# A 2D Haar inverse, by rows: sixteen of 64 channels by TensorE products, forty-eight by VectorE butterflies

## The chip, the core and the metric

The kernel runs on one core of one Trainium2 chip. The metric is the device time of one execution in microseconds. Before the change the median of three runs is 2953.84 us (2952.67 to 2955.11).

## What is computed

The input is a batch of 4 images with 64 channels of 256 x 256 float32. Four layers follow one another: two long convolutions, a Haar layer, and a third long convolution. Cut to what matters:

```python
def conv(x, hx, hy, bias):            # layers 0, 1 and 3
    k = einsum('ijk,imk->ijmk', hx, hy)   # the 2D filter is a product of two 1D filters
    y = irfft2(rfft2(x, 512) * rfft2(k, 512) / 512)[..., :256, :256]
    return y + x * bias

def haar_layer(x, v, conv_w, tau):    # layer 2
    f1 = haar2d(x)                    # 1D Haar along rows, then along columns
    acc = 0
    for i in range(2):
        f4 = einsum('bchw,oc->bohw', f1 * v[i], conv_w[i])      # mixes the channels
        acc = acc + sign(f4) * relu(abs(f4) - tau[i])
    return haar2d(acc, inverse=True) + x
```

As each filter is a product of two 1D filters, the kernel computes a convolution as two products of an image with triangular Toeplitz matrices, one for each axis. hx and hy come from small sine networks.

## The kernel before, in words

**Stages.** A channel's image is a tile of 128 partitions x 512. For each batch the kernel does three things in turn.

1. Convolutions (function `convolutions`), one channel after another: load x and the Toeplitz tile `t` (L237), product `a0` (tile pa), ACT copy (L260), product `y0` (tile py), residual sum on DVE (L277), the same again for the second layer (`a1`, `y1`). Then `pairs` takes sums and differences of neighbouring columns (L322, L323), `store` keeps them in DRAM (`keep`), `levels` does the rest of the row transform, and `split`, `rest`, `down` and `away` do the column transform: an ACT copy rounds to float32r (L354), DVE subtracts for the remainder (L359), and TensorE multiplies both with a sign matrix (tile pz, L366). The result goes to DRAM (`coef`).
2. Mixing (function `mixing`), 64 groups g: load four coefficient rows of all channels, multiply with the channel matrix (tile px, L434), scale (L453 on DVE, L458 on ACT), absolute value (L462) and sign (L465) on ACT, threshold and product with the sign on DVE (L469, L473), and add (L479) into the large tile `z`. `z` is 128 partitions x (4 chunks of 16 channels) x 128 places x 16 channels; place_of gives the place of a row.
3. Inverse (function `inverse`): the column transform is done in place in `z` by butterflies on DVE. `halve` (L284, L285) subtracts and then forms 2 x even - odd; `level(n, chunk, ...)` does one level of one chunk of 16 channels, with n = 1, 2, 4, ..., 64; levels 32 and 64 are cut in parts of 16, so that a chunk has 7 wide pairs of 128x1024 (n = 16, two parts of 32, four of 64) and four narrow ones. Then for each channel c: `early` loads r from `keep` (L512) and the Toeplitz tile, `fetch` copies one channel out of `z` (tile zc, L519), `rows` multiplies and transposes (tile pw, L526, L527), `join` adds r and takes sums and differences (tiles t and u, L533, L536, L537), and the third convolution follows (`a3`, `y3` on tiles pa, py; output on ACT's DMA queue, L573). For batches 0 to 2, a third of the channels is put off: `aside` stores u in `late`, and `convolution` does them beside the mixing of batch 3.

**Order.** Nothing runs in loops over time. Each step of each unit is an event with a time in ticks (`at`), the tick of its unit plus an offset from the table `PLACE`; the events are sorted and issued in that order (L630). The tile framework then sets the final order on each engine by its own schedule, in which a later step can stand in a gap of its engine ahead of an earlier one, and it adds the waits. The convolutions of batch b+1 run beside the mixing of batch b; the inverse of batch b comes after its mixing, with the tail of the convolutions in it. In `inverse`, `along` is the first tick of the batch's mixing, `start` that of its inverse, and `turn` is 16 ticks ahead of the chunk's own first channel.

**Buffers.** PSUM: four banks of tag "mm" (pa, py, pz, pw) and two pairs for px. SBUF: five Toeplitz tiles, three of tag "f" (r, and the coefficient rows), two of tag "f4", two of tag "co" (y3 and the coefficients on their way out).

Of the kernel before, what the change touches and what calls it, by code (L numbers as in the profile page):

```python
# [9 lines left out]
F32 = mybir.dt.float32  # L10
F32R = mybir.dt.float32r
AF = mybir.ActivationFunctionType
ALU = mybir.AluOpType
# [3 lines left out]
B, C, S, EMB, ORD = 4, 64, 256, 33, 64  # L17
P = 128
# [7 lines left out]
PLACE = {  # L26
    "load": 0.714,
    "a0": 1.643,
    "a0 copy": 1.643,
    "y0": 2.571,  # L30
    "y0 sum": 2.571,
    "a1": 3.5,
    "a1 copy": 3.5,
    "y1": 4.429,
# [15 lines left out]
    "shrink": 1.777,  # L50
    "signed": 2.802,
    "add": 3.331,
    "early": -0.4,
    "fetch": 0.414,
    "rows": 1.071,
    "join": 1.433,
    "aside": 2.357,
    "a3": 2.47,
# [37 lines left out]
def conv_seq_kernel(ctx, tc, x, fz, fw, bias, decay, haar, haar_row, factors, vt, taut, wmix, out):  # L96
# [14 lines left out]
    nc = tc.nc  # L111

    const = ctx.enter_context(tc.tile_pool(name="const", bufs=1))
# [1 line left out]


    zpool = ctx.enter_context(tc.tile_pool(name="zpool", bufs=1))
    tp = ctx.enter_context(tc.tile_pool(name="toep", bufs=5))
    io = ctx.enter_context(tc.tile_pool(name="io", bufs=2))
    mx = ctx.enter_context(tc.tile_pool(name="mx", bufs=2))  # L120
    psm = ctx.enter_context(tc.tile_pool(name="psm", bufs=4, space=PSUM))
# [2 lines left out]

    hbt = const.tile([P, P], F32, name="hbt")
    hbr = const.tile([P, P], F32R, name="hbr")
    hrow = const.tile([P, 2, P], F32, name="hrow")
    hsinv, ident = hrow[:, 0, :], hrow[:, 1, :]
    wb = const.tile([P, 2, P], F32, name="wb")
# [3 lines left out]
    z = zpool.tile([P, 4, P, 4, 16], F32, name="z")  # L133
# [71 lines left out]
        return [load, *steps, end, warm]  # L205

    def constants():
        nc.sync.dma_start(hbt, haar)
        nc.sync.dma_start(hrow, haar_row)
        nc.vector.memset(wb, 0.0)  # L210
        for r in range(2):
            nc.sync.dma_start(wb[r * C : (r + 1) * C, r, :], wmix)
        nc.scalar.copy(hbr, hbt)
# [90 lines left out]
    def at(time, run, unit):  # L304
        events.append((time, len(events), run, unit))
# [104 lines left out]
    def mixing(b, start, n_act):  # L410

        st = {}

        def load(g):
            f = mx.tile([P, 2, S], F32, name=f"f_{b}_{g}", tag="f", bufs=3)
            nc.sync.dma_start(f, coef[b].rearrange("k c p w -> (k c) p w")[:, 2 * g : 2 * g + 2])
            st[g] = {"f": f}
            if g % GT == 0:
                t = mx.tile([P, 2, GT, 16], F32, name=f"vt_{b}_{g}", tag="vt")
                nc.sync.dma_start(t, scales[g // GT])  # L420
                st["vt", g // GT] = t

        def scale(g, i):
            return st["vt", g // GT][:, i, g % GT, :]

        def over(g, i, n):
            return scale(g, i)[:, :n].unsqueeze(2).to_broadcast([P, n, C])

        def mix(g):
            f = st[g]["f"]  # L430
            ps = psx.tile([P, 2, 2, S], F32, name=f"px_{b}_{g}", tag="mix")
            for q in range(2):
                for h in range(2):
                    nc.tensor.matmul(  # L434
                        ps[:, q, h, :],
                        f[:, q, h * P : (h + 1) * P],
                        wb.rearrange("p r n -> p (r n)"),
                        start=True,
                        stop=True,
                    )  # L440
            if g == 0:

                one, two = ps[:, 0, :, :P], ps[:, 0, :, P:]
                d = mx.tile([P, 2, P], F32, name=f"d_{b}", tag="mag")
                nc.vector.tensor_copy(d, two)
                nc.vector.tensor_sub(two, one, d)
                nc.vector.tensor_add(one, one, d)
            st[g]["f4"] = mx.tile([P, 16, C], F32, name=f"f4_{b}_{g}", tag="f4")
            st[g]["px"] = ps.rearrange("p q h (r i o) -> p (q h r i) o", r=2, i=2)

        def scaled(g):
            px, n = st[g]["px"], 16 - n_act
            nc.vector.tensor_tensor(st[g]["f4"][:, :n], px[:, :n], over(g, 0, n), ALU.mult)  # L453

        def scaled_too(g, half):
            px, f4 = st[g]["px"], st[g]["f4"]
            for j in range(16 - n_act + half * (n_act // 2), 16 - (1 - half) * (n_act - n_act // 2)):
                nc.scalar.mul(f4[:, j], px[:, j], scale(g, 0)[:, j : j + 1])  # L458

        def size(g):  # L460
            mag = st[g]["mag"] = mx.tile([P, 16, C], F32, name=f"mag_{b}_{g}", tag="mag")
            nc.scalar.activation(mag, st[g]["f4"], AF.Abs)  # L462

        def sign(g):
            nc.scalar.activation(st[g]["f4"], st[g]["f4"], AF.Sign)  # L465

        def shrink(g):
            mag = st[g]["mag"]
            nc.vector.tensor_sub(mag, mag, over(g, 1, 16))  # L469

        def signed(g):
            mag = st[g]["mag"]
            nc.vector.scalar_tensor_tensor(mag, mag, 0.0, st[g]["f4"], ALU.max, ALU.mult)  # L473

        def add(g):
            parts = st.pop(g)["mag"].rearrange("p (q x i) (n c) -> p q i x n c", q=2, i=2, n=4)
            for q in range(2):
                slot = place_of(2 * g + q)
                nc.vector.tensor_add(  # L479
                    z[:, :, slot].rearrange("p n x c -> p x n c"), parts[:, q, 0], parts[:, q, 1]  # L480
                )

        def place_of(i):

            n = 1 << i.bit_length() - 1 if i else P
            return (2 * (i - n) + 1) * (P // 2 // n) if i else 0

        for g in range(S // 4):
            for name, stage in zip(
                ("mix load", "mix", "scaled", "scaled too", "scaled rest", "size", "sign", "shrink", "signed", "add"),  # L490
                (
                    load,
                    mix,
                    scaled,
                    lambda g: scaled_too(g, 0),
                    lambda g: scaled_too(g, 1),
                    size,
                    sign,
                    shrink,
                    signed,  # L500
                    add,
                ),
            ):
                at(start + g + PLACE[name if b + 1 < B else "l " + name], stage, g)

    def inverse(b, start, put_off):

        st = {}

        def early(c):  # L510
            r = mx.tile([P, 2, 2, P], F32, name=f"r_{b}_{c}", tag="f", bufs=3)
            nc.sync.dma_start(r, keep[b][c])  # L512
            st[c] = {"r": r}
            if c not in put_off:
                st[c][2] = toeplitz(2, c, f"t2_{b}_{c}")

# [5 lines left out]
        def rows(c):  # L522
            a = st[c]["z"]
            ps = psm.tile([P, 2, 2, P], F32, name=f"pw_{b}_{c}", tag="mm")
            for m in range(2):
                nc.tensor.matmul(ps[:, 0, m, :], a[:, 0, m, :], hsinv, start=True, stop=True)  # L526
                nc.tensor.transpose(ps[:, 1, m, :], a[:, 1, m, :], ident)  # L527
            st[c]["pw"] = ps

        def join(c):  # L530
# [14 lines left out]
        def when(tick, n, chunk, *span):  # L545
            at(tick + PLACE["level"], lambda _: level(n, chunk, *span), 0)

        at(along + 11 + PLACE["level"], lambda _: butterfly(), 0)
        for chunk in range(4):
            beside = b + 1 < B or chunk == 0  # L550
            turn = start + 16 * (chunk - 1)
            for n in (1, 2, 4, 8):
                when(along + 12 + chunk if beside else turn, n, chunk)
            when(along + 22 + 2 * chunk if beside else turn + 1, 16, chunk)
            for i in range(2):
                when(along + 38 + 4 * chunk + 2 * i if beside else turn + 2 + 2 * i, 32, chunk, 16 * i, 16)
            for i in range(4):
                when(turn + 4 + 3 * i if chunk else along + 43 + 8 * i - (i == 3), 64, chunk, 16 * i, 16)

        for c in range(C):  # L560
            for name, stage in zip(("early", "fetch", "rows", "join"), (early, fetch, rows, join)):
                at(start + c + PLACE[name], stage, c)
            if c in put_off:
                at(start + c + PLACE["aside"], aside, c)
            else:
                for name, stage in zip(("a3", "a3 copy", "y3", "y3 sum", "out"), last(b, st)):
                    at(start + c + PLACE[name], stage, c)

    def last(b, st):
        return [  # L570
# [45 lines left out]
    start = ready + 3  # L616
# [12 lines left out]
        ahead = start - 3  # L629
    for _, _, stage, unit in sorted(events, key=lambda e: e[:2]):  # L630
        stage(unit)


def _haar_order():
# [101 lines left out]
```

## Time and profile before

| what | value |
|---|---|
| median of three runs | 2953.84 us |
| the profiled execution's own time | 2959.32 us |
| its span | 2957.5 us |
| PE busy | 2826.3 us (96%), 16438 matmuls |
| DVE busy | 2529.3 us (86%) |
| ACT busy | 2056.6 us (70%) |
| POOL busy | 361.2 us (12%) |
| DMA | 649.69 MB, mean 220 GB/s |
| mean granted clock of TensorE | 0.992 |
| mixing of batch 1 (first px to first zc) | 1096 to 1550 us |
| inverse of batch 1 (first zc to next px) | 1550 to 1767 us |

The span is the time from the first to the last instruction in the profile. Busy is the union of the instructions of an engine. A matmul's record lasts from its start to a modelled end and overlaps the next one, so busy PE is more than the work it does. A float32 product stands in the trace as two matmul records. A row of a group of instructions gives line, engine, operation, tiles, shapes, count, busy time, mean duration in ns, and the idle time of the engine ahead of it with what ended it. In a list of stretches the columns are from:to, length, then busy time and count of each engine, the granted clock, the share of the DMA engines and GB/s.

### The profile page before, as it was taken

How to read it: one execution, taken by the hardware profiler on the slowest of the kernel's cores; microseconds unless marked ns; L12 is line 12 of the kernel's file. 1: busy time of each engine (PE TensorE's matmuls, PEld its weight loads, DVE VectorE, ACT ScalarE, POOL GpSimd, SP SyncE). 2: the span in 40 equal slices, each digit the busy share in tenths (PEclk: the TensorE clock that was granted, in tenths of full speed). 3: DMA queues.
4: the chain of work that ended last, by engine and by line, in shares of the span. 5: the costliest groups of instructions: out<-in, count | busy, mean ns of one | idle time of the engine just before them, and what ended most of it. 6: DMA issues, size and time to landing. Idle time of an engine off the chain costs nothing. (4 is left out here: it accounts for less than half of the span.)

```text
span 2957.5 us, 52078 instructions
## 1 busy us (share of the span) xinstructions
PE 2826.3 (96%) x16438; PEld 2541.0 (86%) x16438; DVE 2529.3 (86%) x4287; ACT 2056.6 (70%) x4885; POOL 361.2 (12%) x644
## 2 busy tenths in 40 slices
PE   8999999999898899999998899999998899998999
PEld 6899998888787898898987798898987798877898
DVE  4655568999998679999998669999998679999986
ACT  2333338999894558999884558999884558887454
POOL 0111111311111001131211001131221000000000
PEclk9999999999999999999999999999999999999999
DMA  5877777666566786777676786777776797767777
GB/s 159 248 231 230 232 235 218 207 201 205 180 204 199 249 264 198 211 215 212 208 215 210 241 271 194 214 211 216 210 209 215 247 280 235 231 200 210 223 237 213
DMA packets 599222, 649.69 MB, mean 220 GB/s; under 512 B 48449, under 2 KB 516900, under 8 KB 598820
## 3 DMA queue, kind: packets, MB, share of 16 engines
q1 hardware_dynamic: 519716, 562.02, 65.0%
q10 hardware_dynamic: 79232, 84.34, 8.1%
q8 instruction: 133, 2.18, 0.3%
q14 instruction: 141, 1.16, 0.1%
HBM read 426.70 MB, written 219.48 MB: 218 GB/s over the span
## 5 line engine op out<-in xcount | busy, mean ns | idle before, releaser
L246 PE MATMUL py<-t,a 128*128 128x256 f32 x3072 | 927.7, 384 | 8.8 <-ACT a L260 8.3
L260 ACT COPY a<-pa 128x512 f32<-128x512 f32 x768 | 490.8, 639 | 482.4 <-PE pa L247 428.9
L458 ACT ACTIVATE f<-px,vt 128x64 f32<-128x64 f32 x2816 | 620.4, 407 | 107.5 <-DVE f L453 105.9
L247 PEld LDWEIGHTS py<-t,a 128*128 128x128 f32 x3072 | 587.6, 191 | 81.3
L247 PE MATMUL py<-t,a 128*128 128x128 f32 x3072 | 593.3, 275 | 0.0
L246 PEld LDWEIGHTS py<-t,a 128*128 128x128 f32 x3072 | 498.2, 193 | 48.3 <-ACT a L260 19.6
L434 PE MATMUL px<-wb,f 128*128 128x256 f32 x2048 | 493.9, 382 | 21.5 <-ACT f L458 21.4
L519 ACT COPY zc<-z 128x512 f32<-128x512 f32 x256 | 281.2, 1100 | 220.8 <-PE pw L527 189.9
L336 POOL TENSOR_TENSOR sd<-less 128x128 f32<-128x128 f32 (+4 forms) x320 | 200.8, 627 | 1899.8 <-DVE less L335 1644.8
L434 PEld LDWEIGHTS px<-wb,f 128*128 128x128 f32 x2048 | 368.8, 191 | 69.2 <-ACT f L458 30.2
L246 PE MATMUL pa<-t,y 128*128 128x256 f32 x1024 | 310.3, 385 | 16.6 <-DVE y L277 10.0
L469 DVE TENSOR_TENSOR mag<-mag,vt 128x1024 f32<-128x1024 f32 x256 | 311.3, 1216 | 7.5 <-ACT mag L462 6.2
L473 DVE SCALAR_TENSOR_TENSOR mag<-mag,f 128x1024 f32<-128x1024 f32 x256 | 311.4, 1217 | 0.6 <-ACT f L465 0.4
L462 ACT ACTIVATE mag<-f 128x1024 f32<-128x1024 f32 x256 | 303.6, 1186 | 11.4 <-DVE z L479 10.1
L246 PE MATMUL pa<-t,x 128*128 128x256 f32 x1024 | 305.8, 380 | 0.9 <-issue 0.9
L246 PE MATMUL pa<-t,u 128*128 128x256 f32 x772 | 241.0, 395 | 61.4 <-issue 42.6
L465 ACT ACTIVATE f<-f 128x1024 f32<-128x1024 f32 x256 | 292.0, 1141 | 3.7
L359 DVE TENSOR_TENSOR sp<-sd,sp 128x512 fp32r<-128x512 f32 x256 | 178.1, 696 | 128.0 <-ACT sp L354 126.5
L277 DVE SCALAR_TENSOR_TENSOR y<-u,bsb,py 128x512 f32<-128x512 f32 x193 | 143.7, 745 | 144.9 <-PE py L247 108.9
L277 DVE SCALAR_TENSOR_TENSOR y<-x,bsb,py 128x512 f32<-128x512 f32 x256 | 189.3, 740 | 46.7 <-PE py L247 45.7
L247 PEld LDWEIGHTS pa<-t,y 128*128 128x128 f32 x1024 | 195.6, 191 | 26.8
L247 PEld LDWEIGHTS pa<-t,x 128*128 128x128 f32 x1024 | 194.6, 190 | 26.3
(66 smaller groups left out, 4400.5 us busy)
## 6 DMA issues: line engine op xcount, KB each, us to landing
t<-pad SPq DMA_DIRECT2D x768, 256.0 KB, 4.1
x<-in_x SPq DMA_DIRECT2D x256, 256.0 KB, 3.9
coef<-co SPq DMA_DIRECT2D x256, 256.0 KB, 3.2
f<-coef SPq DMA_DIRECT2D x256, 256.0 KB, 3.1
r<-keep SPq DMA_DIRECT2D x256, 256.0 KB, 3.9
out_y<-y ACTq DMA_DIRECT2D x256, 256.0 KB, 3.8
keep<-sums SPq DMA_DIRECT2D x256, 128.0 KB, 2.8
keep<-sd SPq DMA_DIRECT2D x256, 128.0 KB, 2.7
```

Source lines behind the costliest of these rows:

```text
L246: nc.tensor.matmul(ps[:, m, :], src[:, 0, m * P : (m + 1) * P], t[:, ::-1], start=True, stop=False)
L247: nc.tensor.matmul(ps[:, m, P:], src[:, 1, m * P : (m + 1) * P], t[:, : P - 1 : -1], start=False, stop=True)
L260: nc.scalar.copy(a, s["p" + new])
L277: nc.vector.scalar_tensor_tensor(y, s[res], bsb[:, layer, c : c + 1], s["p" + new], ALU.mult, ALU.add)
L336: engine.tensor_tensor(t[:, :, :, half:length], v[..., 0], v[..., 1], ALU.subtract)
L434: nc.tensor.matmul(ps[:, q, h, :], f[:, q, h * P : (h + 1) * P], wb.rearrange("p r n -> p (r n)"), start=True, stop=True,)
L458: nc.scalar.mul(f4[:, j], px[:, j], scale(g, 0)[:, j : j + 1])
L462: nc.scalar.activation(mag, st[g]["f4"], AF.Abs)
L465: nc.scalar.activation(st[g]["f4"], st[g]["f4"], AF.Sign)
L469: nc.vector.tensor_sub(mag, mag, over(g, 1, 16))
L473: nc.vector.scalar_tensor_tensor(mag, mag, 0.0, st[g]["f4"], ALU.max, ALU.mult)
L519: nc.scalar.copy(a.rearrange("p h k i -> p (h k) i"), z[:, c // 16, :, :, c % 16].rearrange("p i x -> p x i"))
```

## The change

The first chunk of each batch (channels 0 to 15) has no butterflies any more. Its column transform is done per channel, between `rows` and `join`, by two new steps. `halves` copies pw to a float32r tile w on ACT and lets DVE subtract for the remainder. `cols` multiplies both parts with a new sign matrix `hb` into a PSUM bank (tile pu), from which `join` reads. `hb` is loaded and rounded once at the start; its rows follow the places in `z`. For these channels `join` and what follows come one tick later. Chunks 1 to 3 keep their butterflies, with other due times: levels 1 to 8 in the mixing (for batch 3 at `turn`), levels 16, 32 and 64 at `turn` + 1 to `turn` + 12. The Toeplitz tile of the third convolution is asked for in a step of its own, `sooner`, 0.4 tick ahead of the load of r, and there are six such tiles, not five. The diff, cut to its core:

```diff
+    "sooner": -0.8,
     "early": -0.4,
     "fetch": 0.414,
     "rows": 1.071,
+    "halves": 1.522,
+    "cols": 2.143,
     "join": 1.433,
...
-    tp = ctx.enter_context(tc.tile_pool(name="toep", bufs=5))
+    tp = ctx.enter_context(tc.tile_pool(name="toep", bufs=6))
...
+    hb = const.tile([P, P], F32R, name="hb")
...
-        nc.sync.dma_start(hbt, haar)
+        signs = part(P)
+        nc.sync.dma_start(hbt, haar[0])
+        nc.sync.dma_start(signs, haar[1])
+        nc.scalar.copy(hb, signs)
...
         def early(c):
             r = mx.tile([P, 2, 2, P], F32, name=f"r_{b}_{c}", tag="f", bufs=3)
             nc.sync.dma_start(r, keep[b][c])
-            st[c] = {"r": r}
+            st[c]["r"] = r
+
+        def sooner(c):
+            st[c] = {}
             if c not in put_off:
                 st[c][2] = toeplitz(2, c, f"t2_{b}_{c}")
...
+        def halves(c):
+            w = st[c]["w"] = mx.tile([P, 2, 2, 2, P], F32R, name=f"w_{b}_{c}", tag="f4")
+            ps = st[c]["pw"]
+            nc.scalar.copy(w[:, 0], ps)
+            nc.vector.tensor_tensor(w[:, 1], ps, w[:, 0].bitcast(F32), ALU.subtract)
+
+        def cols(c):
+            ps = psm.tile([P, 2, 2, P], F32, name=f"pu_{b}_{c}", tag="mm")
+            flat = "p e m w -> p (e m w)"
+            for i in range(2):
+                nc.tensor.matmul(
+                    ps.rearrange(flat), hb, st[c]["w"][:, i].rearrange(flat), start=(i == 0), stop=(i == 1)
+                )
             st[c]["pw"] = ps
...
-        for chunk in range(4):
-            beside = b + 1 < B or chunk == 0
+        for chunk in range(1, 4):
             turn = start + 16 * (chunk - 1)
             for n in (1, 2, 4, 8):
-                when(along + 12 + chunk if beside else turn, n, chunk)
-            when(along + 22 + 2 * chunk if beside else turn + 1, 16, chunk)
+                when(along + 12 + 3 * chunk if b + 1 < B else turn, n, chunk)
+            when(turn + 1, 16, chunk)
             for i in range(2):
-                when(along + 38 + 4 * chunk + 2 * i if beside else turn + 2 + 2 * i, 32, chunk, 16 * i, 16)
+                when(turn + 2 + 2 * i, 32, chunk, 16 * i, 16)
             for i in range(4):
-                when(turn + 4 + 3 * i if chunk else along + 43 + 8 * i - (i == 3), 64, chunk, 16 * i, 16)
+                when(turn + 6 + 2 * i, 64, chunk, 16 * i, 16)
...
+            turn = start + c
+            if c < 16:
+                at(start + c + PLACE["halves"], halves, c)
+                at(start + c + PLACE["cols"], cols, c)
+                turn += 1
+            at(turn + PLACE["join"], join, c)
```

More of the change, by code (lines that the diff above doesn't have):

```diff
@@ L477, in add @@
             for q in range(2):
-                slot = place_of(2 * g + q)
+                to = slot(2 * g + q)
                 nc.vector.tensor_add(
-                    z[:, :, slot].rearrange("p n x c -> p x n c"), parts[:, q, 0], parts[:, q, 1]
+                    z[:, :, to].rearrange("p n x c -> p x n c"), parts[:, q, 0], parts[:, q, 1]
                 )
-        def place_of(i):
-            n = 1 << i.bit_length() - 1 if i else P
-            return (2 * (i - n) + 1) * (P // 2 // n) if i else 0
         for g in range(S // 4):
@@ L527, in rows @@
                 nc.tensor.transpose(ps[:, 1, m, :], a[:, 1, m, :], ident)
+            st[c]["pw"] = ps
+        def halves(c):
[10 more added lines that the diff above has]
+                )
             st[c]["pw"] = ps
@@ L548, in inverse @@
         at(along + 11 + PLACE["level"], lambda _: butterfly(), 0)
-        for chunk in range(4):
-            beside = b + 1 < B or chunk == 0
+        for chunk in range(1, 4):
             turn = start + 16 * (chunk - 1)
             for n in (1, 2, 4, 8):
-                when(along + 12 + chunk if beside else turn, n, chunk)
-            when(along + 22 + 2 * chunk if beside else turn + 1, 16, chunk)
+                when(along + 12 + 3 * chunk if b + 1 < B else turn, n, chunk)
+            when(turn + 1, 16, chunk)
             for i in range(2):
-                when(along + 38 + 4 * chunk + 2 * i if beside else turn + 2 + 2 * i, 32, chunk, 16 * i, 16)
+                when(turn + 2 + 2 * i, 32, chunk, 16 * i, 16)
             for i in range(4):
-                when(turn + 4 + 3 * i if chunk else along + 43 + 8 * i - (i == 3), 64, chunk, 16 * i, 16)
+                when(turn + 6 + 2 * i, 64, chunk, 16 * i, 16)
         for c in range(C):
-            for name, stage in zip(("early", "fetch", "rows", "join"), (early, fetch, rows, join)):
+            for name, stage in zip(("sooner", "early", "fetch", "rows"), (sooner, early, fetch, rows)):
                 at(start + c + PLACE[name], stage, c)
+            turn = start + c
[4 more added lines that the diff above has]
+            at(turn + PLACE["join"], join, c)
             if c in put_off:
-                at(start + c + PLACE["aside"], aside, c)
+                at(turn + PLACE["aside"], aside, c)
             else:
                 for name, stage in zip(("a3", "a3 copy", "y3", "y3 sum", "out"), last(b, st)):
-                    at(start + c + PLACE[name], stage, c)
+                    at(turn + PLACE[name], stage, c)
     def last(b, st):
@@ L631, in conv_seq_kernel, with slot @@
         stage(unit)
+def slot(i):
+    if i == 0:
+        return 0
+    n = 1 << i.bit_length() - 1
+    return (2 * (i - n) + 1) * (P // 2 // n)
 def _haar_order():
@@ L718 @@
         "decay": _decay(),
-        "haar": lay(signs.T),
+        "haar": lay(np.stack([signs.T, signs[np.argsort([slot(i) for i in range(P)])]])),
         "haar_row": lay(np.stack([scaled, np.eye(P, dtype=np.float32)], axis=1)),
```

## The prediction

> **What bounds the kernel now.** I read the totals first, then stages, then the work inside a stage, then single steps. The page's totals (PE 96%, DVE 86%, ACT 70%) mix four kinds of stage, so I cut the span where the first px product (L434) and the first zc copy (L519) of each batch start. Columns: from:to, length, busy of PE, PEld, DVE, ACT, POOL with counts, clock, DMA share, GB/s.
>
> ```profile
> 451.00:884.00 433.00, 418.26 (x2284) 367.20 (x2283) 421.53 (x709) 410.11 (x1233) 80.84 (x130) 1.00 0.67 200
> 884.00:1096.00 212.00, 188.99 (x1194) 172.22 (x1193) 158.45 (x288) 108.76 (x133) 12.90 (x20) 0.96 0.77 242
> 1096.00:1550.00 454.00, 452.25 (x2544) 407.19 (x2543) 443.36 (x741) 398.34 (x1121) 95.23 (x140) 1.00 0.71 209
> 1550.00:1767.00 217.00, 196.06 (x1221) 177.76 (x1220) 162.06 (x295) 111.57 (x138) 12.71 (x20) 0.95 0.78 242
> 2429.00:2733.00 304.00, 285.28 (x1517) 250.94 (x1515) 300.00 (x422) 248.02 (x575) 0.00 (x0) 0.99 0.74 220
> 2733.00:2957.50 224.50, 216.35 (x1432) 200.94 (x1432) 185.07 (x318) 108.39 (x129) 0.00 (x0) 1.00 0.75 224
> ```
>
> These are mixing 0, inverse 0, mixing 1, inverse 1, mixing 3, inverse 3 (batch 2 repeats batch 1: 454 and 208 us). Busy PE overlaps itself, so I count PE by distance between starts. The timeline rows below give it: a 256-column pass 0.216 us (two in 0.43), a 128-column pass 0.11, two 512-column float32r passes 0.54 (1643.60 to 1644.14). A contraction is 4 x 0.216 + 4 x 0.11 = 1.30 us, a px group 8 x 0.216 = 1.73, pw 6 x 0.11 = 0.66.
>
> ```profile
> 1642.80 0.39 PE L247 MATMUL py<-t,a 128*128 128x128 f32 x2
> 1643.02 0.60 PE L246 MATMUL py<-t,a 128*128 128x256 f32 x2
> 1643.45 0.39 PE L247 MATMUL py<-t,a 128*128 128x128 f32 x2
> 1643.60 0.71 PE L366 MATMUL pz<-sp,hbr 128*128 128x512 f32 x2
> 1644.14 0.38 PE L526 MATMUL pw<-hrow,zc 128*128 128x128 f32 x2
> ```
>
> With the counts per tile in each stage, PE's own work is: mixing 1, 64 px + 52 pz pairs + 241 contractions = 110.7 + 28.1 + 314 = 453 of 454: PE is full. Mixing 0, 208 contractions: 411 of 433, with DVE at 422 and ACT at 410, three engines close together. Mixing 3, 125 contractions: 274 of 304, but DVE 300: DVE is full. Inverse 1, 64 pw + 12 pz + 101 contractions: 181 of 217. Inverse 3, 131 contractions: 213 of 224.5, PE nearly full. Now inside an inverse stage:
>
> ```profile
> 1550.00:1605.00 55.00, 46.70 (x261) 41.17 (x260) 53.05 (x84) 23.20 (x32) 12.71 (x20) 0.91 0.65 201
> 1605.00:1700.00 95.00, 82.99 (x510) 74.27 (x509) 60.54 (x117) 51.61 (x65) 0.00 (x0) 0.95 0.77 238
> 1700.00:1767.00 67.00, 66.37 (x454) 62.32 (x453) 48.47 (x96) 36.76 (x43) 0.00 (x0) 1.00 0.92 282
> 2740.00:2860.00 120.00, 117.95 (x781) 109.20 (x780) 118.81 (x197) 59.60 (x72) 0.00 (x0) 1.00 0.77 230
> ```
>
> The first 55 us (channels 0 to 9) are DVE's: 53 busy, with butterflies in between, while PE has some 40 us of work and a clock of 0.91. The next 95 wait here and there, the last 67 are PE's. In inverse 3 (last line) both are full.
>
> **What the skill says.** "Trainium Kernel Development and Optimization", Performance Expectations: matmul busy time is a bad measure because matmuls are pipelined; here a 128-column pass shows 275 ns and starts every 110, so it agrees. "VectorE: DVE Perf Modes", Mode 1x: fp32 with two tensors, or PSUM, gets one result a cycle (0.96 GHz, 533 ns for 512, an estimate); the trace has 0.60 us between starts for 512, from SBUF (L359) and from PSUM (L533) alike. "TensorE: Matmul & The Clock Gate", Architectural detail: VectorE and ScalarE queues are strict FIFO; so the built program's order on each engine, which I read, is the order of execution. Same page, Part 1: idle lowers the clock to half for a while; the 0.91 above and passes at twice the distance near 1652 us agree.
>
> **The change part by part.** Costs come from these rows and from distances between starts.
>
> ```profile
> L284 DVE TENSOR_TENSOR z<-z 128x1024 f32<-128x1024 f32 x112 | 135.9, 1218 | 0.1
> L354 ACT CAST sp<-sd 128x512 fp32r<-128x512 f32 x256 | 186.1, 727 | 10.4 <-POOL sd L336 10.4
> L359 DVE TENSOR_TENSOR sp<-sd,sp 128x512 fp32r<-128x512 f32 x256 | 178.1, 696 | 128.0 <-ACT sp L354 126.5
> 1592.86 2.35 DVE L284 TENSOR_TENSOR z<-z 128x1024 f32<-128x1024 f32 x2
> 1595.13 1.21 DVE L285 SCALAR_TENSOR_TENSOR z<-z 128x1024 f32<-128x1024 f32 x1
> ```
>
> Two L284 take 2.27 from start to start, so a wide pair (L284 + L285) costs DVE 2.27.
>
> Removed per batch: chunk 0's butterflies, 7 wide pairs (15.9 us) and four narrow (2 x (0.135 + 0.20 + 0.335 + 0.60) = 2.5): 18.4 of DVE. Added per batch on 16 channels: an ACT copy (between starts 0.52: 8.3 us), a DVE subtract (0.60: 9.6), a product in two passes (0.54: 8.7 of PE). In all DVE -35, PE +35, ACT +33.
>
> Where it lies is not what the ticks say: the scheduler pulls butterflies forward into gaps. Wide pairs in the built order, before and after: mixing 0 18 and 15, mixing 1 and 2 17 and 17, mixing 3 6 and 1; behind the last mixing group 10 and 6, 11 and 4, 11 and 4, 22 and 20. So most butterflies stay in mixing; "in the inverse ticks" is true of few.
>
> - Mixing 0: 3 pairs and the narrow ones, -9.3 of DVE, in its second half, where DVE is the fullest. ACT (410) and PE (411) stand 12 us behind it: -6, bounds -9 and 0.
> - Mixing 1, 2: -2.5 of DVE, but PE is full and keeps its work: -1 each, bounds -3 and 0. The cover here is PE itself.
> - Mixing 3: 5 pairs, -11.4 on the bounding engine; PE is 30 below. Some of its waits on PE stay: -9, bounds -11.4 and -5.
> - Inverse 0, 1, 2: up to channel 8, DVE loses about 12 us net in 1 and 2 (7 pairs less, some 8 subtracts more), 5 in 0 (4 pairs), and PE gains 8 x 0.54 = 4.3 of work that fits in its 15 idle us: -7 (in 0: -4). Channels 8 to 15: PE +4.3 and a subtract each; PE is at some 85% there: +4. The later tick of the join shifts work behind channel 16, +1. Sum +1 (inverse 0), -2, -2; bounds -8 and +8 each.
> - Inverse 3: PE is 95% full and DVE too: 16 x 0.54 = 8.7 lands on the path: +8.5, bounds +5 and +12.
> - Added waits: pu waits for the subtract, which waits for the copy, which waits for pw; behind pu in PE's queue stand the next contraction and pw. Between pw and its pu the built order has the previous pu, one or two contractions and the next pw: 0.54 + 1.30 to 2.6 + 0.66 = 2.5 to 3.8 us. The chain: 0.73 copy + 0.70 subtract + 0.68 (the previous join, in front of it) + some 0.2 between = 2.3. It fits, with little to spare. I take 0, bounds 0 and 0.5 a channel. PSUM: four banks now serve four tiles a tick, not three; each is needed back after its reader that PE waits for anyway: 0.
> - DMAs: t is loaded 0.4 tick earlier, in front of r on SP's queue, and has six buffers; r waits behind it only for issue (about 0.4 us). The groups by form have 3.9 us of pa waiting on t in all, and the inverse's PE gaps end with u (L537), not with t: 0, bounds -4 and +2. The second sign matrix (64 KB, one copy) lies under the batch-0 convolutions: 0; without cover some 4 us.
>
> Sum: -6 - 2 - 9 + 1 - 4 + 8.5 = -11.5. The profiled execution took 2959.3 (span 2957.5 and 1.8 around it), which becomes 2947.8; the median of the runs, 2953.8, is 5.5 lower and becomes **2942**.
>
> **Rivals.** (1) Forecast, 2942, own range 2928 to 2948: chance 0.43. (2) More: mixing 0 and 3 give all (-9, -11), each inverse 0 to 2 keeps PE busy from its start and regains clock (-8), mixing 1 and 2 -1 each, inverse 3 +6: -40, 2914. For it speaks clock 0.91 in the first 55 us; against it the 95 us after them, whose waits on output buffers stay. Chance 0.14. (3) Even: mixing 0 is held by ACT and PE (0), mixing 3 gives 8, inverse 3 costs 8, the rest cancels: 2954. Chance 0.17. (4) Slower: the chain pw, copy, subtract, pu does not fit, since a y3 sum (L277) in front of the subtract waits for an output buffer (22.4 us of such waits, on coef<-co, in the group of y<-u among the groups by form) or a zc copy (1.10) stands in front of the ACT copy. PE then stands in each of 64 channels; it decides from 11.5 / 64 = 0.18 us a channel; at 0.5 it costs 32: 2974. Chance 0.26. That all butterflies really moved to the inverse ticks would cost tens of us, but the built order excludes it.
>
> **Numbers.** Within 0.2% (5.9 us) counts as no change, about what a measurement can tell. Faster 0.57 (1, 2), same 0.17, slower 0.26. Range 2916 to 2980: it holds 1 and 3, most of 4 and the edge of 2.
>
> **What would show it.** Mixing 1 and 2 within 3 us of 454; mixing 3 near 295 with DVE still above PE; zc of channel 8 in inverse 1 some 40 us after the first (now 47.4: 1550.1 to 1597.5); inverse 3 near 233 with 3.8 us a channel up to 16 (now 3.28). Wrong would be: pu as a line of PE's waits above 10 us, a mixing stage that moves by over 5 us for its new order alone, or a longer middle of the inverse stages.

## The result and the profile after

| | before | after |
|---|---|---|
| median of the runs | 2953.26 us (2952.66 to 2955.11, 4 runs) | 2913.1 us (2911.86 to 2913.15, 4 runs) |
| span of the profiled execution | 2957.5 us | 2911.3 us |
| granted clock | 0.992 | 0.997 |

The ratio is 0.9862, 95% interval 0.9845 to 0.9879: 40 us less, where 11.5 less were forecast. The time lies 3 us below the range of the prediction and on its rival (2).

The stages of the changed kernel, cut in the same places as before the change: mixing 0, inverse 0, mixing 1, inverse 1, mixing 3, inverse 3.

```profile
448.40:866.20 417.80, 409.37 (x2257) 361.23 (x2257) 408.85 (x690) 407.09 (x1230) 79.72 (x130) 1.00 0.68 205
866.20:1075.60 209.40, 195.75 (x1257) 179.00 (x1256) 161.91 (x301) 117.97 (x153) 8.00 (x20) 0.98 0.79 248
1075.60:1526.40 450.80, 448.57 (x2522) 404.05 (x2521) 439.04 (x730) 398.52 (x1121) 88.06 (x140) 1.00 0.70 209
1526.40:1733.50 207.10, 196.35 (x1275) 180.12 (x1274) 159.19 (x301) 119.51 (x156) 7.37 (x20) 0.99 0.82 256
2385.60:2675.70 290.10, 279.33 (x1514) 247.81 (x1512) 286.33 (x410) 245.79 (x575) 0.00 (x0) 1.00 0.78 232
2675.70:2911.30 235.60, 225.82 (x1464) 209.44 (x1464) 191.53 (x324) 116.11 (x145) 0.00 (x0) 0.99 0.68 210
```

Every stage but the last is shorter than in the rows of the prediction, and the inverse stages have their clock back (0.96 and 0.95 before). Where three engines stood close together in mixing 0, they still do, in a stage that is 15 us shorter.

One caution on these cuts. The first zc copy is a moment on ACT, and the change moves it against PE's work. The VectorE rows of the timeline at the start of inverse 1, before the change:

```profile
1545.00 0.41 DVE L479 TENSOR_TENSOR z<-mag 128x256 f32<-128x256 f32 x1
1545.33 1.21 DVE L285 SCALAR_TENSOR_TENSOR z<-z 128x1024 f32<-128x1024 f32 x1
1546.47 1.21 DVE L284 TENSOR_TENSOR z<-z 128x1024 f32<-128x1024 f32 x1
...
1548.86 1.21 DVE L285 SCALAR_TENSOR_TENSOR z<-z 128x1024 f32<-128x1024 f32 x1
1550.00 0.73 DVE L277 SCALAR_TENSOR_TENSOR y<-x,bsb,py 128x512 f32<-128x512 f32 x1
```

And after it:

```profile
1525.07 0.41 DVE L486 TENSOR_TENSOR z<-mag 128x256 f32<-128x256 f32 x1
1525.40 1.21 DVE L292 SCALAR_TENSOR_TENSOR z<-z 128x1024 f32<-128x1024 f32 x1
```

Before, the last addition into z ends at 1545.4 and butterflies follow; the copy of channel 0 starts at 1550.1, when the last of them has ended. After, it starts at 1526.4, 0.9 us behind the end of the last addition. From the end of the last px to the first zc there were 19.1 us (in a second profile of the kernel before, E1 below) and are 15.5. PE was busy all of both, so the 3.6 us are convolutions that now lie behind the first zc, where PE used to stand. The comparison below is therefore cut at the last px, not at the first zc.

### The profile page after: what moved, and what is told of

Read it like the earlier page. It is cut to its first block, busy times and chain, and to the rows that moved or that the text cites. A ratio compares the mean times of both kernels' runs of the same rounds, so it can differ in the third digit from the quotient of the medians.

```text
span 2911.3 us, 52368 instructions
## 1 busy us (share of the span) xinstructions
PE 2827.3 (97%) x16566; PEld 2551.1 (88%) x16566; DVE 2499.0 (86%) x4263; ACT 2085.2 (72%) x4950; POOL 329.7 (11%) x644
## 5 line engine op out<-in xcount | busy, mean ns | idle before, releaser
L253 PEld LDWEIGHTS py<-t,a 128*128 128x128 f32 x3072 | 496.2, 191 | 47.5 <-ACT a L267 16.8
L343 POOL TENSOR_TENSOR sd<-less 128x128 f32<-128x128 f32 (+4 forms) x320 | 189.3, 592 | 1884.7 <-DVE less L342 1616.8
L254 PEld LDWEIGHTS pa<-t,y 128*128 128x128 f32 x1024 | 194.7, 190 | 26.5
```

The costliest lines, as they stand in the source:

```text
L253: nc.tensor.matmul(ps[:, m, :], src[:, 0, m * P : (m + 1) * P], t[:, ::-1], start=True, stop=False)
L254: nc.tensor.matmul(ps[:, m, P:], src[:, 1, m * P : (m + 1) * P], t[:, : P - 1 : -1], start=False, stop=True)
L343: engine.tensor_tensor(t[:, :, :, half:length], v[..., 0], v[..., 1], ALU.subtract)
```

## The experiments

Stage lengths from the traces, in us. Mixing runs from the first px to 2 us behind the first px of the last group; "to 8" from there to the zc of channel 8; the others between zc copies, and to the next px or the end. The profile of the prediction was 5.5 us above its median, so "before" here is a second profile of it (E1). The runs come from several chips: the kernel before took 2954 us on that of E1, E2, E4 and E5, 2961 on that of E6 to E9, and 2959 on that of E3 and E11 to E13. A ratio compares kernels on one chip, the columns of the table go across chips. Inverse 3 of kernels that leave it alone agrees across the first two within 0.5 us (E1 240.5, E6 240.0).

```
                 before  change  e4     e5     e6     e8     e11    e13    e12
                 (E1)            none   added  due    later  later3 old3   32 ch
start             449.8   448.4  450.0  451.1  450.5  453.4  448.9  449.2  448.0
mixing 0          409.7   398.1  400.1  408.0  399.6  409.1  400.0  399.3  396.6
  to 8             71.4    65.4   67.3   65.0   71.1   67.3   64.5   63.7   57.0
  8 to 15          22.5    24.8   22.9   24.9   26.5   23.0   25.2   24.3   24.4
  16 on           140.0   138.8  139.9  141.1  140.7  140.3  140.9  140.0  142.4
mixing 1          434.9   435.3  435.4  435.2  434.6  435.2  435.5  435.3  433.9
  to 8             65.4    56.9   57.4   64.5   66.0   66.3   56.9   56.9   57.2
  8 to 15          23.4    23.9   20.7   25.1   22.9   23.8   23.9   23.9   23.9
  16 on           141.7   141.8  142.2  145.9  143.0  146.0  144.0  141.7  144.0
mixing 2          434.9   435.3  435.5  435.2  434.6  435.2  435.4  435.3  433.7
  to 8             65.9    56.9   59.1   63.0   66.1   65.4   56.9   56.9   57.2
  8 to 15          23.4    23.9   20.9   25.1   24.4   22.9   23.9   23.9   23.9
  16 on           139.4   136.0  139.3  140.6  138.5  139.4  140.5  139.2  137.1
mixing 3          287.8   277.3  277.6  287.9  287.8  288.1  277.4  287.8  277.1
  inverse 3       240.5   248.4  237.8  253.7  240.0  243.9  243.7  239.4  247.8
```

"16 on" of batches 0 to 2 moves by several us from profile to profile of stages that no edit touches (136 to 146), and single differences there are not read.

### E1: the kernel before, once more

> The kernel before, unchanged, for the spread of its stages from one profiled execution to another. The first profile of it took 5.5 us more than the median of its runs. Theory: the wait of ACT for POOL near 800 us, which costs mixing 0 about 10 us, is the program's own and stands in this profile too, mixing 0 again near 433 us, mixing 1 and 2 at 454. Rival: it is an accident of that execution, and mixing 0 is near 423 here.

2952.63 us. The 5.5 us of the first profile lay in channels 16 to 39 of inverse 1 (78.9 us there, 73.4 here). The stretch of mixing 0 that is looked at below takes 37 us in the first profile and 38 in this one, so it belongs to the program, as the theory had it.

### E2 to E5: the parts alone

E4 takes the butterflies of chunk 0 away and puts nothing in their place: the column transform of channels 0 to 15 is left out.

```diff
-        for chunk in range(4):
+        for chunk in range(1, 4):
```

> The kernel before without the butterflies of chunk 0; the column transform of channels 0 to 15 is left out, and nothing takes its place. The other due times and the Toeplitz loads are those of before. Theory (the whole gain is VectorE work that is gone, and the products cost only in inverse 3): 2953 - 40 - 9 = 2904 us, bounds 2896 and 2912; mixing 0 down by some 15 us, mixing 3 by 11, channels 0 to 8 of inverse 1 and 2 by 9 each. Rival (the gain comes from new due times of chunks 1 to 3 or from the earlier Toeplitz loads): at most 15 us under 2953, so 2938 or more.

2907.96 us, ratio 0.985 (0.9819 to 0.9882). The relief alone gives nearly all that the change gives in the mixing stages and up to channel 8 (table). So the 40 us come from work taken off VectorE and from the order that this leaves, not from anything that the new steps do.

E5 keeps all butterflies and adds the new steps to the kernel before; channels 0 to 15 are transformed twice.

```diff
+            if c < 16:
+                at(start + c + PLACE["halves"], halves, c)
+                at(start + c + PLACE["cols"], cols, c)
+                turn += 1
```

> The kernel before with all its butterflies, and the two new steps (copy and subtract, product by the sign matrix, join a tick later) done for channels 0 to 15 on top of them, so that these channels are transformed twice. Theory (the products are free where PE waits anyway, and cost 8.7 us in inverse 3): 2953 + 9 to + 20, because the 16 subtracts a batch (9.6 us) now also come on top in the first ticks of the inverse, where VectorE is full: 2968. The prediction's rival 4 (chain of pw, copy, subtract, pu holds PE): 0.5 us a channel more, 2985 or above. If the products cost nothing anywhere: 2956 or less.

2967.38 us, ratio 1.0051 (1.0032 to 1.0069): 13 us in all, and inverse 3 alone takes 13.2 more. In the other three inverses some 26 us of work on PE, 25 on ACT and 29 on DVE (by the prediction's prices) add 2 us by the table.

E2 has only the Toeplitz part in the kernel before, E3 is the change without it:

```diff
+    "sooner": -0.8,
...
-    tp = ctx.enter_context(tc.tile_pool(name="toep", bufs=5))
+    tp = ctx.enter_context(tc.tile_pool(name="toep", bufs=6))
```

> The kernel before with one part of the change alone: the Toeplitz tile of the third convolution asked for 0.4 tick ahead of r, and six such tiles. Theory: no wait for t bounds anything, 2953 within 4 us. Rival (t was what the inverse waited for between channels 16 and 40): inverse 0 to 2 shorter by 3 to 8 us each, 2930 to 2944.

> The changed kernel with the Toeplitz part undone: the tile is asked for together with r again, behind it, and there are five tiles. The Toeplitz part alone on the kernel before gave a ratio of 0.9988. Theory (it is worth the same small amount here): ratio to the kernel before 0.987 to 0.989, against 0.9862 for the change. Rival (the products need it, because PE then waits for t more): 0.991 or above.

E2: 2951.09 us, ratio 0.9988 (0.9981 to 0.9995), 3 us. E3: 2927.06 us, ratio 0.9891 (0.9875 to 0.9908) where the change has 0.9862: some 8 us, with intervals that overlap a little. It is a small part and not quite nothing. In E3's trace PE waits 4.6 us in all for t ahead of pa, in the change's 1.2; which waits make up the rest these runs don't show. E4, E5 and E2 together make -46 + 13 - 3 = -36 of the 40. The due times (E6, -9) are not added to it: most of what they gain lies in a place where E4 gains too.

### E6 and E7: the order in mixing 0

E6 keeps all butterflies and gives only chunks 1 to 3 the due times of the change.

```diff
-            when(along + 22 + 2 * chunk if beside else turn + 1, 16, chunk)
+            when(turn + 1 if chunk else along + 22, 16, chunk)
```

> The kernel before with all its butterflies and no products; only the due times of the butterflies of chunks 1 to 3 are those of the change. Theory (work that is gone, not its order, makes the gain): 2953 within 6 us, and mixing 0 not more than 4 us shorter. Rival (the order makes the gain of the first channels of inverse 1 and 2): channels 0 to 8 there shorter by over 5 us each, 2940 or less.

2951.67 us where the kernel before took 2960.75 on that chip, ratio 0.997 (0.9958 to 0.9982). Neither the theory nor the rival held: the theory allowed mixing 0 to be 4 us shorter, and the rival's gain in the first channels of inverses 1 and 2 did not come. Mixing 0 is 10.1 us shorter, though all the butterflies are still there. The gain sits in one place, the four groups from 52 to 56. That stretch in the kernel before (E1), in E6, in E4 and in the change:

```profile
779.70:817.80 38.10, 30.79 (x160) 26.66 (x160) 31.88 (x52) 30.66 (x94) 7.74 (x10) 0.96 0.50 147
```

```profile
779.30:808.20 28.90, 27.51 (x152) 24.03 (x151) 28.48 (x48) 28.56 (x88) 10.38 (x10) 1.00 0.69 202
```

```profile
782.60:808.70 26.10, 25.57 (x144) 22.80 (x143) 26.09 (x44) 24.91 (x76) 9.84 (x10) 1.00 0.68 199
```

```profile
778.80:805.30 26.50, 25.84 (x144) 22.71 (x143) 26.39 (x44) 26.43 (x83) 8.13 (x10) 1.00 0.65 197
```

In the first row PE, DVE and ACT each stand for 6 to 8 of 38 us; in the other three DVE is full. What they stand for is in the timeline of the first profile of before:

```profile
792.17 3.33 POOL L336 TENSOR_TENSOR sd<-less 128x128 f32<-128x128 f32 x1 [31.73 <-DVE less L335]
...
798.92 0.62 ACT L354 CAST sp<-sd 128x512 fp32r<-128x512 f32 x1 [2.62 <-POOL sd L336]
799.45 3.17 ACT L458 ACTIVATE f<-px,vt 128x64 f32<-128x64 f32 x15
802.46 1.99 PE L434 MATMUL px<-wb,f 128*128 128x256 f32 x8 [2.45 <-ACT f L458]
803.59 1.22 DVE L469 TENSOR_TENSOR mag<-mag,vt 128x1024 f32<-128x1024 f32 x1 [3.22 <-ACT mag L462]
```

POOL gets its input from DVE late and needs 6.7 us for its levels; ACT's next instruction is the rounding copy that waits for POOL (2.62 us), and the 15 scalings behind it in ACT's queue wait along, though their input is there (the px products ahead of them ended at 793.2); px waits for the scalings, and DVE for what follows on ACT.

Why POOL's input is late is in DVE's rows of the same timeline, where a wide pair stands directly ahead of the row level that POOL waits for:

```profile
788.67 1.22 DVE L284 TENSOR_TENSOR z<-z 128x1024 f32<-128x1024 f32 x1
789.81 0.42 DVE L322 TENSOR_TENSOR sums<-y 128x256 f32<-128x256 f32 x1
790.14 1.22 DVE L285 SCALAR_TENSOR_TENSOR z<-z 128x1024 f32<-128x1024 f32 x1
791.28 0.42 DVE L323 TENSOR_TENSOR sd<-y 128x256 f32<-128x256 f32 x1
791.62 0.42 DVE L335 TENSOR_TENSOR less<-less 128x256 f32<-128x256 f32 x1
```

In E6 the same row level comes 8 us earlier, and the next wide pair behind it:

```profile
783.56 0.42 DVE L335 TENSOR_TENSOR less<-less 128x256 f32<-128x256 f32 x1
...
790.46 1.21 DVE L284 TENSOR_TENSOR z<-z 128x1024 f32<-128x1024 f32 x1
```

The pair shown takes some 2.3 us of these 8. Another pair stands before it (its instructions start at 779.47 and 780.94), where E6 has none between 776.6 and 790.5; the rest is other VectorE work that comes in another order.

E7 tries the cure on the kernel before: the rounding copies come a tick later. The line for `rest` changes in the same way.

```diff
-                at(after(end + 3 + j, n) + PLACE["split"], split, c)
+                at(after(end + 3 + j, n) + 1 + PLACE["split"], split, c)
```

> The kernel before with one edit: split and rest (the ACT copy to float32r and the VectorE subtract ahead of pz) come one tick later, so that ACT's copy doesn't stand in its queue ahead of scaling work while POOL still works on the row transform. Theory (mixing 0 lost some 10 us near 800 us because that copy waited for POOL, whose input came late from a full VectorE): mixing 0 shorter by 5 to 10 us, the rest as before, 2943 to 2949. Rival (mixing 0 is held by VectorE's and ACT's sums alone): mixing 0 within 2 us of 409.

2954.22 us, ratio 0.9979 (0.9971 to 0.9988), with mixing 0 only 2.7 us shorter. Groups 52 to 56 now take 23.5 us:

```profile
787.90:811.40 23.50, 22.55 (x127) 20.03 (x125) 23.49 (x37) 20.67 (x65) 7.94 (x10) 1.00 0.74 225
```

They hold less work than before (127 matmul records for 160), so the length alone says little. But DVE, which stood for 6.2 of 38.1 us before, is full in them once the copies come later, so the account of the waiting copy holds for that place. Groups 0 to 52 take 337.6 us (329.9 before) and mixing 1 and 2 are 5 and 3 us longer: moving every copy lengthens other places. As a cure the theory failed; as an account of the one place it stands.

### E8, E9, E11: the join one tick later

E8 has no product. Only `join` and what follows come a tick later for channels 0 to 15 of the kernel before.

```diff
+            turn = start + c + (1 if c < 16 else 0)
+            at(turn + PLACE["join"], join, c)
```

> The kernel before with one edit: join and all that follows it comes one tick later for channels 0 to 15, without the products. The kernel with products on top of the butterflies was 6 us faster than before in channels 0 to 8 of inverse 0 although it did more work there. Theory A (the later join does that, because TensorE has a tick more of other work between pw and the product that needs u): channels 0 to 8 of inverse 0 shorter by 5 to 7 us, of inverse 1 and 2 by 2 to 5, in all 2938 to 2945. Theory B (it was another order of the convolutions' tail there): inverse 0 within 2 us, 2950 to 2956.

2961.84 us, ratio 1.0004 (0.9997 to 1.0011). Neither theory held as a whole: channels 0 to 8 are 4.1 us shorter in inverse 0 (A had 5 to 7, B at most 2) and within 1 us of before in inverses 1 and 2, and the time stays the same. Inverse 3 takes 3.4 us more, and the place is the step back: counted from the start of the inverse, channel 15 now has its join at tick 17.4, and so has channel 16. PE's waits in E8 from the zc of channel 16 to that of channel 40:

```profile
PE pa L246 <- issue: 2.0, 2, 1.3
PE pa L246 <- DVE u L537: 2.0, 1, 2.0
PE pa L246 <- PE pw L527: 0.5, 2, 0.3
```

The change has the same three waits, 2.0, 2.0 and 0.5 us, in the same stretch; the kernel before has only the third, 1.0 us. In both traces each of the two waits that are put down to "issue" ends 0.1 us after a u is written, so 4.0 of the 4.5 us are waits for u: DVE makes two joins in one tick and the next convolution is late.

E9 takes the step back away in the change, for all batches, by moving `turn += 1` out of the condition; E11 only for batch 3, with this edit:

```diff
-                turn += 1
+            if c < 16 or b + 1 == B:
+                turn += 1
```

> The changed kernel with one edit: the join comes a tick later for all 64 channels, not for the first 16 alone. TensorE waits there some 10 us per inverse 0 to 2 between channels 16 and 40 for u. Theory A (a tick more between pw and join lets TensorE go on): channels 16 to 40 shorter by 3 to 8 us in inverse 0 to 2, 2890 to 2905. Theory B (those waits come from the output buffers of y3, which the edit leaves as they are): 2913 within 5 us.

> The changed kernel with the join a tick later for all 64 channels of batch 3, as it is for the first 16; batches 0 to 2 as in the change. Theory (in inverse 3 some 4 of the 8 us that the change adds are the step back at channel 16, where two joins and two channels' products fall into one tick, and not the product itself): inverse 3 shorter by 3 to 5 us, ratio 0.984 to 0.986. Rival (all 8 us are the products' 8.7 us on PE): inverse 3 as in the change, the last channel even a tick later, 0.986 to 0.988.

E9: 2924.4 us, ratio 0.9885 (0.9868 to 0.9901). Inverse 3 is 4.2 us shorter than in the change. In inverses 0 to 2 channels 16 to 39 are 3 to 6 us shorter and the last 24 some 6 us longer, and mixing 1 and 2 are 1.8 us longer and mixing 3 2.8. So the stretch that theory A names did shorten, and its total of 2890 to 2905 did not come. E11: inverse 3 is 4.7 us shorter, and of the waits in that stretch this is left:

```profile
PE pa L253 <- issue: 0.6, 3, 0.2
```

E11's time is 2918.6 us, ratio 0.986 (0.9841 to 0.9879), the same as the change's: the gain inside the stage is shown, a gain in the whole is not.

### E12, E13: how far it carries

E12 does the first 32 channels of batches 0 to 2 by products; E13 leaves batch 3 in its old form.

```diff
-        for chunk in range(1, 4):
+        first_chunk = 1 if b + 1 == B else 2
+        for chunk in range(first_chunk, 4):
...
-            if c < 16:
+            if c < 16 * first_chunk:
```

> The changed kernel with the product for the first 32 channels of batches 0 to 2 (chunks 0 and 1; chunks 2 and 3 keep their butterflies), batch 3 as in the change. Theory (VectorE held only the first 8 channels of an inverse stage, and 4 wide pairs are left there; mixing 1 and 2 are PE's): channels 0 to 8 of inverse 1 and 2 shorter by another 3 to 6 us, channels 16 to 40 longer by 3 to 6 each, in all 2907 to 2922, ratio 0.984 to 0.989. If the products still hide wholly: 0.981 or less. If PE is the bound now: 0.991 or above.

```diff
-            if c < 16:
+            if c < 16 and b + 1 < B:
```

> The changed kernel with batch 3 in the old way: chunk 0 by butterflies at the due times of before, no products there. Theory (in batch 3 the change gains some 10.5 us in mixing 3 and gives 8 back in inverse 3): mixing 3 back at 288, inverse 3 at 240, ratio 0.987 to 0.988 against 0.9862. Rival (the two stages trade nothing but the place of a boundary, and batch 3 gains nothing or loses): 0.986 or less.

E12: 2908.19 us, ratio 0.9838 (0.9814 to 0.9862), the lowest of the study among the kernels that do all the work, but its interval overlaps that of the change. The gain that was forecast for channels 0 to 8 of inverses 1 and 2 is not there (57.2 us for 56.9); it came in inverse 0 (57.0 for 65.4). In inverse 1 the stretch from the first zc to that of channel 8 is now PE's:

```profile
1514.40:1559.60 45.20, 43.39 (x270) 39.45 (x269) 37.29 (x67) 24.65 (x39) 2.91 (x11) 1.00 0.79 237
```

E13: 2919.45 us, ratio 0.9868 (0.9851 to 0.9885), not told from the change: mixing 3 is 10.5 us longer than in the change and inverse 3 is 9.0 shorter, the two stages that its theory named. So nearly the whole gain comes from batches 0 to 2.

## Why the prediction came out as it did

Predicted and measured (E1 to the change), with the prediction's terms put on the cuts of the table:

| step | predicted | measured |
|---|---|---|
| start | 0 | -1.4 |
| mixing 0 | -6 | -11.6 |
| up to channel 8, inverses 0, 1, 2 | -4, -7, -7 | -6.0, -8.5, -9.0 |
| channels 8 to 15 | +4, +4, +4 | +2.3, +0.5, +0.5 |
| behind channel 16 | +1, +1, +1 | -1.2, +0.1, -3.4 |
| mixing 1, 2 | -1, -1 | +0.4, +0.4 |
| mixing 3 | -9 | -10.5 |
| inverse 3 | +8.5 | +7.9 |
| sum | -11.5 | -39.5 |

By the prediction's own cuts, at the first zc, the same gain reads: mixing 0 -16.8, mixings 1 and 2 -3.2 each, mixing 3 -13.8, inverses 0 to 2 +0.3, -4.3 and -8.3, inverse 3 +11.3. There mixing 0 misses by most, 10.8 us, and all four mixing stages and inverse 2 lie outside their bounds. Of each mixing stage's gain 3 to 5 us are the move of the first zc that is described above, which the prediction did not foresee.

**What held.** Most butterflies stay in the mixing, PE-full mixings 1 and 2 give nothing, mixing 3 follows DVE, whose busy time up to the first zc fell by 13.7 us (300.00 to 286.33) while that stretch fell by 13.9. Channel 8 of inverse 1 follows the first zc by 41.5 us (some 40 said). Up to channel 8 the mechanism was right and the size 5.5 us short over three batches. In inverse 0 the cause is not separated, since the relief alone (E4) and the later join alone (E8) take 4.1 us each. The first eight channels of inverse 1 before (E1), with the next eight in the second row:

```profile
1547.40:1593.80 46.40, 38.51 (x224) 34.19 (x223) 45.33 (x72) 19.06 (x28) 10.32 (x14) 0.93 0.68 204
1593.80:1617.20 23.40, 19.46 (x130) 17.51 (x128) 18.30 (x34) 12.74 (x16) 2.68 (x7) 1.00 0.82 248
```

And after:

```profile
1526.40:1567.80 41.40, 38.87 (x242) 35.05 (x241) 38.28 (x67) 22.42 (x35) 4.97 (x10) 1.00 0.75 227
1567.80:1591.70 23.90, 23.90 (x156) 21.93 (x155) 20.46 (x40) 16.45 (x24) 2.40 (x10) 1.00 0.73 242
```

In the first rows DVE goes from 45.33 of 46.40 to 38.28 of 41.40, PE does 18 matmuls more in 5 us less, at the full clock. E6, E8 and E2, which leave the butterflies, leave this stretch as it was in inverses 1 and 2; E4 takes 8.0 and 6.8 us from it. How much of the 5 us is VectorE and how much the clock (0.93 before) no run separates.

**A step that failed: "Channels 8 to 15: PE +4.3 and a subtract each; PE is at some 85% there: +4".** The second rows show this stretch of inverse 1: PE was idle for 3.9 of 23.4 us, took in 26 more matmuls (16 of them products), and is busy 23.90 of 23.90; the stretch grew by 0.5. E4, with neither butterflies nor products for these channels, splits this in two:

```profile
1573.00:1593.70 20.70, 19.07 (x130) 17.53 (x128) 15.10 (x31) 12.74 (x15) 0.18 (x2) 1.00 0.90 281
```

The relief of VectorE takes 2.7 us from the stretch (2.5 in inverse 2, nothing in inverse 0), and from E4 to the change it grows by 3.2 (3.0 and 1.9), where the products were priced at 4.3; the later join alone (E8) moves it by at most 0.5. The step put the relief at nothing: the prediction counted all seven pairs of inverses 1 and 2 ahead of channel 8. In the first profile of before three butterfly instructions start behind the zc of channel 8 (1597.5) in inverse 1:

```profile
1598.04 1.26 DVE L285 SCALAR_TENSOR_TENSOR z<-z 128x1024 f32<-128x1024 f32 x1
...
1601.15 1.21 DVE L284 TENSOR_TENSOR z<-z 128x1024 f32<-128x1024 f32 x1
...
1602.96 1.21 DVE L285 SCALAR_TENSOR_TENSOR z<-z 128x1024 f32<-128x1024 f32 x1
```

Inverse 2 has as many there, inverse 0 none, and after the change none is left in any of the three. The step also charged PE's work in full although PE had gaps, which is the argument that the prediction used one line earlier, for the first eight channels. In all it is 8.7 us over three batches. Behind channel 16, "+1" was not seen; the 7.5 us between sum and trace there lie within what these stretches vary by, and how much of them is real stays open.

**The other step that failed: "ACT (410) and PE (411) stand 12 us behind it: -6".** It is 5.6 us short in the table and 10.8 by the prediction's own cut. The stage was priced as a sum of busy times, with the next engine as its floor. What went is another thing: a single place, four groups that fell from 38.1 to 26.5 us, because DVE's order changed there. E6 shows that it goes with all the butterflies kept. The prediction's own mark for "wrong" was a mixing stage that moves by over 5 us for its new order alone: E6's mixing 0 does, by 10.1.

**Inverse 3: right size, wrong sum.** The forecast put 8.7 us of products on a full PE. Measured, it splits in two. From E8 to the change, which adds the products and drops chunk 0's butterflies, the first zc follows the last px 3.0 us sooner, channels 0 to 15 take 6.9 more and the rest 0.6 more: +4.5. From E1 to E8 the later join costs 3.4, by the waits shown. Undoing the step back gives 4.2 to 4.7. The mark "3.8 us a channel up to 16" failed with it: those channels went from 50.9 to 54.8 us, 3.4 each (before it was 3.18, not the 3.28 of the mark), and channels 16 to 39 from 80.8 to 88.1. That +8.5 and +7.9 agree is partly chance.

**DMAs and Toeplitz tiles: "0, bounds -4 and +2".** E2's 3 us lie inside the bounds, and E3 points to more. The zero was too cautious by 0.1 to 0.3% of the time.

**The rivals.** Rival (2) named what happened in the inverses, PE busy from the start and the clock regained; the prediction held against it that the waits of the later 95 us stay, and that is nearly so (from channel 16 to 39 of inverse 1 PE is idle for 9.5 of 73.4 us in E1 and for 8.0 of 75.0 after) and beside the point, since most of the gain lies ahead of them. Its -8 an inverse is -4.9, -7.9 and -11.9 by the table. That its sum of -40 meets the -39.5 is in part chance: its -9 for mixing 0 is again VectorE's sum, and not the one place. Rival (4), the chain from pw to pu, did not come. The groups of the changed kernel by form:

```profile
L546 PE MATMUL pu<-w,hb 128*128 128x512 f32 x128 | 45.8, 439 | 0.0
L540 DVE TENSOR_TENSOR w<-pw,w 128x512 fp32r<-128x512 f32 x64 | 43.7, 683 | 1.3 <-ACT w L539 1.2
L554 DVE SCALAR_TENSOR_TENSOR t<-r,pu 128x512 f32<-128x512 f32 x64 | 43.7, 682 | 7.1 <-PE pu L546 6.8
L539 ACT CAST w<-pw 128x512 fp32r<-128x512 f32 x64 | 37.6, 588 | 50.0 <-PE pw L533 48.0 <-DVE u L558 1.4
```

PE's idle time ahead of pu is 0.0 in all 64 channels, against 32 us that the rival needed; the subtract waits 1.3 us for the copy in all and the join 6.8 for pu, in 14 cases. The chain itself in inverse 1, from the timeline:

```profile
1581.22 0.39 PE L532 MATMUL pw<-hrow,zc 128*128 128x128 f32 x2
...
1582.14 0.58 ACT L539 CAST w<-pw 128x512 fp32r<-128x512 f32 x1 [0.83 <-PE pw L533]
1582.65 0.68 DVE L554 SCALAR_TENSOR_TENSOR t<-r,pu 128x512 f32<-128x512 f32 x1
1583.25 0.68 DVE L540 TENSOR_TENSOR w<-pw,w 128x512 fp32r<-128x512 f32 x1
...
1584.71 0.71 PE L546 MATMUL pu<-w,hb 128*128 128x512 f32 x2
```

The copy starts as pw ends, the join of the channel before stands ahead of the subtract as foreseen, the remainder is there at 1583.9, and pu starts at 1584.7, behind work that PE has anyway. About 0.8 us are to spare.

**What stays open.** Why the schedule of the kernel before puts a wide pair ahead of the row level in that one place was not followed up. Most of the waits that the Toeplitz part shortens are not known. That E12 is faster than the change is not shown.

## What to carry to other kernels

Price a move of work stretch by stretch, by the gaps of the engine that takes it and by what the relieved engine gives back there, and look up in the trace where the removed work stands: here products priced at 4.3 us cost 3.2 in a stretch that the relief alone made 2.7 shorter, so that it grew by 0.5. Where three engines have almost the same busy time and none is full, look for a place where all stand at once before taking the next engine's busy time as the floor: one copy at the head of a queue cost 10 of 410 us. When a step of some units is moved by a tick, look at the unit where the shift ends, since two steps fall into one tick there.

## What was not expected of the hardware

An ACT copy of 512 elements to float32r took 588 ns from PSUM (w from pw) and 732 ns from SBUF (sp from sd). The DVE subtraction to float32r took 683 ns with an operand in PSUM and 700 ns with both in SBUF. "VectorE: DVE Perf Modes", Specifications, in the Trainium skill has ScalarE closer to PSUM and VectorE closer to SBUF; the trace agrees for ScalarE, and shows no such gain for VectorE in this operation. The chain in the prediction took the copy by its SBUF row, 0.14 us too long.
